# A two-layer graph network on one core: the last product by seven quarter products, with an order of its own for each end

## The chip, the core and the metric

The kernel runs on one core of one Trainium2 chip. Its engines are TensorE (PE, with its weight loads shown apart as PEld), VectorE (DVE), ScalarE (ACT), GpSimd (POOL) and SyncE (SP), which here issues nearly all transfers. The metric is the device time of one execution in microseconds, lower is better.

## The reference

64 graphs of 256 nodes with 256 features, and an integer 256 x 256 adjacency for each, all in float32, pass two blocks. The first has two graph attentions and a feed-forward, the second an eight-head attention with a value weight for each relation, and a feed-forward:

```python
h = gat(x, adj, W1, a1); h = gat(h, adj, W2, a2)       # softmax over axis 1, masked by adj > 0
h = ln(x + h, g_ln1, b_ln1)
y = ln(h + relu(h @ w_ff1 + b_ff1) @ w_ff2 + b_ff2, g_ln2, b_ln2)
q, k = y @ Wq + bq, y @ Wk + bk                        # 8 heads of 32
attn = softmax(q k^T / sqrt(32))
out = sum over r of (attn * (adj == r)) @ (y @ Wv[r] + bv[r])
c = ln(y + out @ Wo + bo, g1, beta1)
d = ln(c + gelu(c @ W1 + b1) @ W2 + b2, g2, beta2)     # W1 256x1024, W2 1024x256
```

## The kernel before

`binary` does the work; it holds for an adjacency of zeros and ones, and `general` follows only if another value was seen. One graph is cut into about 180 pieces, small functions kept under names in a dictionary (`graph`, L762). `L` loads, `G` does both graph attentions and the first layer norm's sums, `F` the first feed-forward, the second norm and q and k, `A` the heads, `T` the output projection, the third norm, the second feed-forward, the last norm and the store.

The order of the work is written out by hand. `PERIOD` (L43) lists all pieces, each with a lag: `F.f0/2` in period n is that piece of graph n - 2. The loop at L791 goes through 69 periods (64 graphs and the largest lag, 5), and runs of each list entry only what exists. Nothing reorders it: each engine meets its instructions, and SP its DMA issues, in this order, and waits at semaphores where data or a buffer is not ready. The first periods and the last ones run the same list with most entries missing.

Names that are needed below:

- `seven_products` (L429): a product of 2 x 2 blocks by seven block products in place of eight. Pieces a to e are on PE and write PSUM banks X, Z and Y; pieces k1 to k4 take a bank out first, p1 to p3 add a bank to what was taken. It needs four sums of blocks of the left side (`S`, made on POOL by `combine`, L414) and of the right side (weights, made once, by `differences`, L153). It is used for both feed-forwards' first product (`F.h*`, `T.h*`) and the values (`A.v*`).
- `out` (L513), pieces `F.f0`, `F.f1`, `T.f0`, `T.f1`: the second product of a feed-forward, plain, eight accumulated matmuls for each half of the nodes, 256 columns wide. A float32 matmul is two instructions in the trace.
- `F.r0` to `r3` and `T.ge0` to `ge3`: bias and relu or gelu on ACT (L509).
- `layernorm` (L354): `ln` (add and statistics on DVE), `rs` (root on POOL), `nm` (DVE); `scaled` (L386): `ra`, `rb`, times weight and plus bias on POOL (L392, L399). A to D are the four norms.
- `turned` (L322): `dt` turns a tile by a transposing DMA, `dm` moves its halves by two DMAs, the join (`c*`, `mg*`, L345) copies on ACT or POOL.
- Heads: `sc` scores, `mx`, `ex` (L685, into a tile `p`, five buffers), `rz`, `sp` (POOL, L698), `dt`, `dm`, `mg`, `pm` (times adjacency, DVE, L713), `o` (L721), `oc`; `T.wo` projects.
- PSUM: all pieces take their tiles from one pool of eight banks (`mm_tile`, L109).
- Setup: `joint_weights` (L215) builds `wx`; `fold_ff`, `column_bias` and `scale_rows` put a norm's weight and bias into the next product's weights (L260 to L267). These stand ahead of the periods; `after` (L307) loads and folds the rest after periods 1 and 2.

## Time and profile before

| what | us |
|---|---|
| median of 3 runs | 3156.15 (3155.87 to 3160.32) |
| the profiled execution | 3158.29 |
| its span | 3156.4 |
| PE busy / DVE / ACT / POOL | 3048.8 / 2459.1 / 2555.5 / 2122.4 |
| mean granted clock of PE | 0.986 |
| bytes by DMA | 449 MB, 142 GB/s |
| matmuls of L517 (both second products) | 466.2 + 455.0 |
| matmuls of L495 (both first products) | 967 |

The span is the time from the first to the last instruction; the time of the execution has a little around it. In the lines below a group is: source line, engine, operation, output <- inputs, shapes, count, then its busy time and the mean of one in ns, then the idle time of its engine just before it and what ended most of that. Matmuls overlap in the pipeline, so the mean of one is longer than the step from one to the next. A tile's letter is the norm whose output it belongs to: `ff_c` and `hid_c` are the second feed-forward's (`T`), `ff_a` the first's.

### The profile page before, as it was taken

To read this page: it belongs to the slowest core of one execution; us is meant where nothing else is said; L and a number is where in the kernel's file an instruction comes from. 1 tells how busy PE (TensorE), PEld (TensorE's weight loads), DVE (VectorE), ACT (ScalarE), POOL (GpSimd) and SP (SyncE) were. 2 spreads that over 40 slices of the span, in tenths; PEclk is the share of its full clock that TensorE was granted. 3 is DMA by queue.
4 is the path that set the end of the run, shared out by engine and by line. 5 is a ranking of instruction groups with operands and counts; after the bars stand their busy time and mean duration, and the time that the engine had idled before them with its cause. 6 is when DMAs were issued, how large, how long until landed. Compare 5 with 4: busy or idle time off the path is not lost.

```text
span 3156.4 us, 64811 instructions
## 1 busy us (share of the span) xinstructions
PE 3048.8 (97%) x21734; PEld 2613.1 (83%) x21734; DVE 2459.1 (78%) x5231; ACT 2555.5 (81%) x5822; POOL 2122.4 (67%) x2990
## 2 busy tenths in 40 slices
PE   5799999999999999999999999999999999999996
PEld 4678888888888888888888888888888888888875
DVE  3578888888888888888887888888888888888763
ACT  1478888888888888888888888888888888888874
POOL 2457667667766766766766776766776676676664
PEclk8899999999999999999999999999999999999998
DMA  4477777778678677777677777777777767777663
GB/s 133 87 140 151 142 148 147 146 142 153 145 148 151 143 143 154 144 148 147 146 143 150 148 145 146 151 141 149 151 143 147 152 141 148 151 143 145 143 128 68
DMA packets 1022849, 449.14 MB, mean 142 GB/s; under 512 B 770960, under 2 KB 1020816, under 8 KB 1022512
## 3 DMA queue, kind: packets, MB, share of 16 engines
q1 hardware_dynamic: 1021248, 442.70, 70.0%
q8 instruction: 175, 2.87, 0.4%
q0 software_dynamic: 976, 1.72, 0.4%
q14 instruction: 162, 1.33, 0.1%
q10 hardware_dynamic: 288, 0.52, 0.1%
HBM read 58.87 MB, written 16.78 MB: 24 GB/s over the span
## 4 chain that ended last, share of the span: by engine, by line
PE 85%; DMA 5%; ACT 3%; DVE 3%; POOL 2%; issue 2%; SPq 0%; ACTq 0%; POOLq 0%; DVEq 0%
PE ff_a L517 13%; PE ff_c L517 12%; PE o L721 7%; PE hX_a L495 7%; PE hX_c L495 6%; PE sc L671 4%; PE vX L645 3%; PE k L632 3%; PE wo L740 3%; PE wh L544 3%; PE q L632 3%; PE gat_b L597 3%; PE hY_c L495 3%; PE gat_a L597 3%; PE hY_a L495 3%; DMA halves_p<-pairs_p 3%
## 5 line engine op out<-in xcount | busy, mean ns | idle before, releaser
L345 ACT COPY pm<-halves_p 128x1024 uint16<-128x1024 uint16 x384 | 516.6, 1346 | 119.6 <-DMA halves_p<-pairs_p 118.6
L713 DVE TENSOR_TENSOR pm<-pm,adj 128x512 f32<-128x512 f32 x512 | 465.4, 926 | 87.4 <-POOL pm L345 63.6
L517 PE MATMUL ff_c<-w_L_gnn_W,hid_c 128*128 128x256 f32 x2048 | 466.2, 381 | 8.4 <-ACT hid_c L509 8.4
L517 PE MATMUL ff_a<-w_L_gnn_w_ff,hid_a 128*128 128x256 f32 x2048 | 455.0, 380 | 2.2 <-ACT hid_a L509 2.2
L517 PEld LDWEIGHTS ff_a<-w_L_gnn_w_ff,hid_a 128*128 128x128 f32 x2048 | 390.6, 191 | 56.4 <-ACT hid_a L509 2.9
L517 PEld LDWEIGHTS ff_c<-w_L_gnn_W,hid_c 128*128 128x128 f32 x2048 | 385.9, 191 | 61.2 <-ACT hid_c L509 10.2
L721 PE MATMUL o<-pm,v 128*32 128x256 f32 x4096 | 249.9, 383 | 1.3 <-ACT pm L345 0.9
L509 ACT ACTIVATE hid_a<-hid_a,col_L_gnn_b_ff 128x256 f32<-128x256 f32 x512 | 218.4, 512 | 12.4 <-DVE hid_a L477 12.4
L345 POOL COPY pm<-halves_p 128x1024 uint16<-128x1024 uint16 x128 | 172.1, 1345 | 81.5 <-DMA halves_p<-pairs_p 74.7
L509 ACT ACTIVATE hid_c<-hid_c,col_L_gnn_b 128x256 f32<-128x256 f32 x512 | 218.3, 496 | 4.9 <-DVE hid_c L477 2.0
L721 PEld LDWEIGHTS o<-pm,v 128*32 128x32 f32 x4096 | 120.7, 110 | 98.5 <-issue 16.7
L425 POOL TENSOR_TENSOR S_a<-cols_a 128x128 f32<-128x128 f32 x128 | 58.5, 457 | 179.2 <-ACT cols_a L345 179.2
L495 PEld LDWEIGHTS hX_a<-cols_a,f_L_gnn_w_ff 128*128 128x128 f32 x1024 | 126.0, 194 | 41.4 <-DVE s_B L573 24.3
L495 PE MATMUL hX_a<-cols_a,f_L_gnn_w_ff 128*128 128x128 f32 x1024 | 144.6, 285 | 13.3 <-ACT cols_a L345 9.2
L671 PE MATMUL sc<-kT,qT 32*128 32x256 f32 x2048 | 149.1, 403 | 1.5 <-ACT qT L642 1.5
L495 PE MATMUL hX_a<-S_a,f_L_gnn_w_ff 128*128 128x128 f32 x1024 | 138.2, 278 | 9.1 <-ACT hid_a L474 9.0
L345 ACT COPY cols_y<-halves_y_y 128x1024 uint16<-128x1024 uint16 x64 | 86.5, 1352 | 74.5 <-DMA halves_y_y<-pairs_y_y 74.4
L632 PE MATMUL k<-cols_y,w_L_gnn_Wk 128*128 128x256 f32 x512 | 127.2, 393 | 18.5 <-ACT cols_y L345 18.5
L495 PE MATMUL hX_c<-S_c,f_L_gnn_W 128*128 128x128 f32 x1024 | 141.7, 281 | 2.2 <-ACT hid_c L474 2.2
L495 PEld LDWEIGHTS hX_a<-S_a,f_L_gnn_w_ff 128*128 128x128 f32 x1024 | 130.0, 192 | 16.7 <-ACT hid_a L474 12.6
L495 PEld LDWEIGHTS hX_c<-cols_c,f_L_gnn_W 128*128 128x128 f32 x1024 | 134.2, 191 | 11.6 <-ACT cols_c L345 4.2
L495 PEld LDWEIGHTS hX_c<-S_c,f_L_gnn_W 128*128 128x128 f32 x1024 | 124.2, 191 | 23.0 <-issue 19.6
(2747 smaller groups left out, 8837.6 us busy)
## 6 DMA issues: line engine op xcount, KB each, us to landing
halves_p<-pairs_p SPq DMA_DIRECT2D x1024, 128.0 KB, 3.3
xT<-in_xT SPq DMA_DIRECT2D x64, 256.0 KB, 4.0
adj<-in_adjT SPq DMA_DIRECT2D x64, 256.0 KB, 4.0
x<-in_x SPq DMA_DIRECT2D x64, 256.0 KB, 3.3
halves_y_a<-pairs_y_a SPq DMA_DIRECT2D x128, 128.0 KB, 3.3
halves_y_y<-pairs_y_y SPq DMA_DIRECT2D x128, 128.0 KB, 3.2
halves_y_c<-pairs_y_c SPq DMA_DIRECT2D x128, 128.0 KB, 3.0
out<-res_d SPq DMA_DIRECT2D x64, 256.0 KB, 2.4
```

The lines of the kernel that those rows point to most:

```text
L345: copy(into().bitcast(U16).rearrange("p (n s) -> p s n", s=2), t["halves"].rearrange("p s k q -> p s (k q)"),)
L495: nc.tensor.matmul(ps[:, f * P : (f + 1) * P], weights()[0][:, factor, f * P : (f + 1) * P], left, start=start and f == 0, stop=f == FC // ...
L509: nc.scalar.activation(tiles["hid"][:, f, :], tiles["hid"][:, f, :], func, bias=b1[:, f : f + 1])
L517: nc.tensor.matmul(tiles["ff"][:, i, :], tiles["hid"][:, f, nodes(i)], weights()[2][:, f, :], start=(f == 0), stop=(f == FC - 1),)
L544: nc.tensor.matmul(t["whp", j], tiles["xT"][:, c, nodes(j)], wx[:, c, :], start=(c == 0), stop=(c == KC - 1),)
L597: nc.tensor.matmul(ps, t["s"][:, j, nodes(i)], t["whz"][:, j, :width], start=(j == 0), stop=(j == NT - 1),)
L632: nc.tensor.matmul(t[key + "p"][:, o, :], w[:, c, nodes(o)], tiles["cols"][:, c, :], start=(c == 0), stop=(c == KC - 1),)
L645: nc.tensor.matmul(ps, left, wv[:, factor, :], start=start, stop=True, skip_group_check=True)
L671: nc.tensor.matmul(t["sc", g, hh][:, i, :], qkv["q"][hd, g, nodes(i)], qkv["k"][hd, g, :], start=True, stop=True,)
L713: nc.vector.tensor_tensor(pm[:, 1, :], pm[:, 0, :], tiles["adj"], ALU.mult)
L721: nc.tensor.matmul(ps[hh * DH : (hh + 1) * DH, :], qkv["v"][:, j, d0 : d0 + DH], t["pm", (g, hh)][:, r, j * N : (j + 1) * N], start=(r == ...
L740: nc.tensor.matmul(t["wo"][:, i, :], t["oT"][:, c, nodes(i)], late["wo"][:, c, :], start=(c == 0), stop=(c == KC - 1),)
```

## The change

- The second feed-forward's second product goes through `seven_products`: pieces `T.fa` to `T.fe` on PE, with 128 columns each, into three PSUM banks. `T.u0` to `u3` make the four sums of the hidden tile's blocks on POOL; the sums of `W2` are made once (`S.p2`). `T.fk*` and `T.fp*` take out and add the banks on DVE; the first takes the residual along.
- The last norm: `ln` only makes statistics; `nm` multiplies by the weight and `rb` by the root with the bias added, both on DVE (`weighted`, `finished`). `T.raD` is gone. The pieces of a period go from 181 to 194.
- `PERIOD` is a new list, run 59 times. `START` (446 entries) and `END` (538) are lists of their own, with each piece's graph written out (negative: from the end).
- Setup becomes pieces `S.*` within `START`, and the late weights' loads (`S.lw`) stand near its front.
- Tiles `p` have four buffers, `S` two; the bank sums of the fold of q and k share one tile.

```diff
 PERIOD = """
-A.dt10/3 F.hk3/2 A.pm01/4 T.hd/5 A.ex13/3 A.mg13/4 A.dm12/3 A.pm02/4 F.hd/2 A.sc0/3 F.hp3/2
...
+G.nmA/1 A.mx13/3 A.rz12/3 F.raB/4 F.sB/3 T.hk3/5 A.mx11/3 A.rz10/3 L.xT/0 T.hp3/5 A.vp2/4 A.dm02/4
+A.pm03/4 G.wh0/0 A.mg02/4 T.hd/5 A.ex13/3 T.hp2/5 G.wh1/0 A.ex11/3 A.sp12/3 A.dm00/4 G.wc0/0
+A.sp10/3 G.wc1/0 A.ve/4 A.pm01/4 F.dtA/1 A.mg00/4 F.dmA/1 F.f1/2 A.pm02/4 G.eA/0 A.pm00/4 T.rbC/5
+F.rbB/4 A.vk4/4 T.he/5 T.ge0/5 A.rz11/3 A.pm11/4 A.rz13/3 A.dt10/3 F.lnB/2 A.sc0/3 A.o0/4 T.ge1/5
+A.mx00/3 G.lrA/0 F.cA/1 T.hk4/5 A.o1/4 T.ge2/5 A.sp11/3 A.sp13/3 A.mx02/3 A.dt12/3 F.ha/1 A.oc0/4
+T.ge3/5 L.adj/0 A.oc1/4 F.sA/1 A.ex00/3 F.hb/1 A.mx03/3 G.away/0 A.dm10/3 A.dm12/3 F.rsB/2 F.hk1/1
+F.hk2/1 T.wo/4 A.mx01/3 G.adA/0 A.mg10/3 T.u0/5 F.hp1/1 T.lnC/4 F.hc/1 T.u1/5 A.mg12/3 A.dt13/3
+G.exA/0 F.raA/1 A.dt11/3 F.nmB/2 A.ex03/3 A.dm13/3 G.rzA/0 T.fa/5 F.hk3/1 A.ex02/3 T.rsC/4 T.fb/5
+F.hd/1 T.nmC/4 G.gA0/0 T.u3/5 T.fk1/5 T.fk2/5 A.rz03/3 A.ex01/3 T.u2/5 F.hp2/1 L.x/0 F.hp3/1
+A.mg13/3 A.sp03/3 G.gA1/0 A.pm12/3 G.wd0/0 G.wd1/0 A.dm11/3 A.rz01/3 T.fc/5 A.va/3 A.vb/3 F.dtB/2
+T.fk3/5 A.mg11/3 F.rbA/1 A.sp01/3 F.r0/1 A.pm13/3 T.dtC/4 A.rz02/3 A.vk1/3 G.eB/0 T.fd/5 F.dmB/2
+T.fp1/5 A.vk2/3 G.lrB/0 T.fp2/5 F.cB/2 F.he/1 A.vc/3 T.dmC/4 T.fe/5 A.rz00/3 F.r1/1 G.adB/0
+A.dt03/3 T.cC/4 A.dt01/3 F.q/2 A.vk3/3 G.exB/0 F.hk4/1 A.vp3/3 T.fp3/5 F.qe0/2 F.k/2 A.sp02/3
+T.fk4/5 F.r2/1 T.ha/4 F.qe1/2 A.dm03/3 F.ke0/2 T.hk1/4 T.lnD/5 G.rzB/0 T.nmD/5 A.sp00/3 T.sC/4
+G.gB/0 A.vp1/3 T.hb/4 A.dm01/3 T.rsD/5 A.dt02/3 T.raC/4 F.ke1/2 T.rbD/5 T.hp1/4 A.sc1/2 T.out/5
+A.dt00/3 G.lnA/0 A.mg03/3 T.hk2/4 F.r3/1 A.mg01/3 A.mx12/2 A.mx10/2 A.vd/3 G.rsA/0 T.hc/4 A.pm10/3
+F.f0/1 A.ex12/2 A.ex10/2
 """.split()
+START = """
+G.away:0 L.adj:2 S.lw:0 S.v0:0 L.adj:1 G.wh0:0 G.wh1:0 G.wc0:0 G.wc1:0 G.eA:0 G.lrA:0 G.adA:0
+S.f0:0 G.exA:0 G.rzA:0 G.gA0:0 G.gA1:0 G.wd0:0 G.wd1:0 S.f1:0 G.eB:0 G.lrB:0 S.f2:0 L.xT:1 G.wh1:1
+G.adB:0 G.wh0:1 L.xT:2 G.exB:0 G.rzB:0 G.wc0:1 G.wc1:1 G.gB:0 G.wh0:2 G.eA:1 G.away:1 G.lrA:1
+G.lnA:0 G.rsA:0 G.nmA:0 G.adA:1 F.dtA:0 F.raA:0 G.exA:1 S.p2:0 S.v1:0 G.wh1:2 S.q0:0 G.wc0:2
...
+END = """
+A.dm02:-4 F.raB:-4 A.vp2:-4 T.hk3:-5 A.pm03:-4 F.sB:-3 A.mx11:-3 A.ve:-4 A.rz12:-3 A.mg02:-4
...
+T.out:-2 T.fe:-1 T.fk4:-1 T.lnD:-1 T.rsD:-1 T.nmD:-1 T.rbD:-1 T.out:-1
+""".split()
...
+    def column_biases(*of, norm):
...
+    def fold_ff(setup, key, ff, norm):
+        half, t = FC // 2, {}
+        def products():
+            def block(c, i):
+                return ff()[0][:, BLOCKS[c, i // half], nodes(i % half)]
+            t["ps"] = column_biases((block, FC), norm=norm())
+        def scales():
+            add_to(ff()[1], t["ps"])
+            scale_rows(lambda c: [ff()[0][:, BLOCKS[c, h], :] for h in range(2)], norm())
+        setup[f"S.{key}0"], setup[f"S.{key}1"] = products, scales
...
+    def out_factors(name):
+        return half_factors(
+            name, FC // 2 * P,
+            lambda c, h: t[name][c * FF // 2 : (c + 1) * FF // 2, nodes(h)].rearrange(
+                "(f p) d -> p f d", p=P
+            ),
         )
...
-    fold_ff(w1, ff0[1], norms[0])
-    differences()
...
-    for w, bias in ((wk, bk), (wq, bq)):
-        column_bias(bias, norms[1], lambda c, i, w=w: w[:, c, nodes(i)], KC)
-        scale_rows(lambda c, w=w: [w[:, c, :]], norms[1])
-    nc.gpsimd.tensor_scalar(bq, bq, QSCALE, 1.0, ALU.mult, ALU.mult)
...
-        late["ff1"] = w1, column("L1_gnn_b1"), weight("L1_gnn_W2", FC)
+        w2, late["out_differences"] = out_factors("L1_gnn_W2")
+        late["w"] = w1, w2
+    def late_rows():
+        late["b1"] = column("L1_gnn_b1")
         for n in ("L1_gnn_g1", "L1_gnn_beta1", "L1_gnn_b2", "L1_gnn_g2", "L1_gnn_beta2"):
             rows[n] = row(t[n], n)
-    def after(period):
-
-        if period == 1:
-            fold_values()
-            late_weights()
-            join_biases(("L0_gnn_b_ln1", "L0_gnn_b_ff2"), ("L0_gnn_b_ln2", "L1_gnn_bo"))
-        elif period == 2:
-            fold_ff(*late["ff1"][:2], norms[2])
-            late["differences"]()
-            join_biases(("L1_gnn_beta1", "L1_gnn_b2"))
+    def ff1():
+        return late["w"][0], late["b1"], late["w"][1]
+    setup = {
+        "S.f2": differences, "S.q0": queries, "S.q1": scaled_queries,
+        "S.v0": value_difference, "S.v1": values, "S.v2": scaled_values, "S.v3": value_differences,
+        "S.lw": late_weights, "S.lr": late_rows, "S.l2": lambda: late["differences"](),
+        "S.j1": lambda: join_biases(("L0_gnn_b_ln1", "L0_gnn_b_ff2"), ("L0_gnn_b_ln2", "L1_gnn_bo")),
+        "S.j2": lambda: join_biases(("L1_gnn_beta1", "L1_gnn_b2")),
+        "S.p2": lambda: late["out_differences"](),
+    }
+    fold_ff(setup, "f", lambda: ff0, lambda: norms[0])
+    fold_ff(setup, "l", ff1, lambda: norms[2])
...
+        def weighted():
+            tiles["res"] = work.tile([P, NT, D], F32, tag="res", name=f"res_{name}", bufs=3)
+            for i in range(NT):
+                nc.vector.scalar_tensor_tensor(
+                    tiles["res"][:, i, :], tiles["acc"][:, i, :], tiles["mv"][:, i, 0:1],
+                    rows[last[0]], ALU.subtract, ALU.mult,
+                )
+        def finished():
+            for i in range(NT):
+                nc.vector.scalar_tensor_tensor(
+                    tiles["res"][:, i, :], tiles["res"][:, i, :], tiles["rstd"][:, i : i + 1],
+                    rows[last[1]], ALU.mult, ALU.add,
+                )
+        do[f"{stage}.ln{key}"], do[f"{stage}.rs{key}"] = sums, root
+        if last:
+            do[f"{stage}.nm{key}"], do[f"{stage}.rb{key}"] = weighted, finished
+        else:
+            do[f"{stage}.nm{key}"] = norm
         return tiles
...
+        def sums(n):
+            if n == 0:
+                h = work.tile([P, 3, FC // 2, P], F32, tag="H", name=f"H_{name}", bufs=1)
+                tiles["H"] = h[:, 0], h[:, 1], hidden(1, 0), h[:, 2]
+            blocks = [hidden(i, h) for i in range(NT) for h in range(2)]
+            engine = nc.gpsimd if ('POOL', 'POOL')[1] == "POOL" else nc.vector
+            add_sums(engine, blocks, tiles["H"], [n])
+        def out_of(ps, factor, left, start):
+            for f in range(FC // 2):
+                nc.tensor.matmul(
+                    ps, left[:, f, :], weights()[2][:, factor, f * P : (f + 1) * P],
+                    start=start and f == 0, stop=f == FC // 2 - 1, skip_group_check=True,
+                )
+        def result(i, h):
+            if "ff" not in tiles:
+                tiles["ff"] = work.tile([P, NT, D], F32, tag="acc", name=f"acc_{name}", bufs=2)
+            return tiles["ff"][:, i, nodes(h)]
+        def begin_result(i, h, ps):
+            nc.vector.tensor_tensor(result(i, h), ps, tiles["res"][:, i, nodes(h)], ALU.add)
+        seven_products(
+            do, stage, "h", name, *by_columns(tiles), into, begin_hidden, hidden, FC // 2 * P
+        )
         for n in range(FC // 2):
             do[f"{stage}.{act}{n}"] = partial(activate, n)
-        for i in range(NT):
-            do[f"{stage}.f{i}"] = partial(out, i)
+        if not seven:
+            for i in range(NT):
+                do[f"{stage}.f{i}"] = partial(out, i)
+            return
+        for n in range(4):
+            do[f"{stage}.u{n}"] = partial(sums, n)
+        seven_products(
+            do, stage, "f", name, hidden, lambda n: tiles["H"][n - 1], out_of,
+            begin_result, result, P,
+        )
...
-            p = t["p", h] = work.tile([P, 2, NT, NT, 64], F32, tag="p", name=f"p_{b}_{g}{hh}", bufs=5)
+            p = t["p", h] = work.tile([P, 2, NT, NT, 64], F32, tag="p", name=f"p_{b}_{g}{hh}", bufs=4)
...
-        feed_forward(do, "T", f"c{b}", c, lambda: late["ff1"], "ge", AF.Gelu)
-        d = layernorm(do, "T", "D", f"d{b}", lambda: (c["ff"], c["res"]))
-        scaled(do, "T", "D", f"d{b}", d, "L1_gnn_g2", "L1_gnn_beta2")
+        feed_forward(do, "T", f"c{b}", c, ff1, "ge", AF.Gelu, seven=True)
+        d = layernorm(
+            do, "T", "D", f"d{b}", lambda: (c["ff"],), ("L1_gnn_g2", "L1_gnn_beta2")
+        )
...
+    lags = max(lag for _, lag in order)
+    def run(piece, b):
+        if piece.startswith("S."):
+            return setup.pop(piece)()
+        if b not in graphs:
+            graphs[b] = {}
+            graph(b, graphs[b], load(graphs[b], b))
+        graphs[b].pop(piece)()
     with tc.manual_schedule(engines={E.PE, E.DVE, E.Activation, E.Pool, E.SP}):
-        for period in range(B + max(lag for _, lag in order)):
-            if 0 < period < B:
-                graphs[period] = {}
-                graph(period, graphs[period], load(graphs[period], period))
+        for entry in START:
+            piece, b = entry.split(":")
+            run(piece, int(b))
+        for period in range(lags, B):
             for piece, lag in order:
-                if do := graphs.get(period - lag, {}).pop(piece, None):
-                    do()
-            after(period)
-        assert not any(graphs.values()), graphs
+                run(piece, period - lag)
+        for entry in END:
+            piece, b = entry.split(":")
+            run(piece, B + int(b))
+        assert not setup and not any(graphs.values()), graphs
```

## The prediction

> **What bounds the kernel now.** I read the page's busy times first, then a table of busy time by stretch, then the timeline of PE inside one period and at both ends. The page says PE 97%, but a busy matmul row is not yet a full PE, so I look for what a period costs.
>
> ```profile
> PE 3048.8 (97%) x21734; PEld 2613.1 (83%) x21734; DVE 2459.1 (78%) x5231; ACT 2555.5 (81%) x5822; POOL 2122.4 (67%) x2990
> PEclk8899999999999999999999999999999999999998
> ...
> L517 PE MATMUL ff_c<-w_L_gnn_W,hid_c 128*128 128x256 f32 x2048 | 466.2, 381 | 8.4 <-ACT hid_c L509 8.4
> ```
>
> The timeline of PE, in the middle of the run (start, length, group, count):
>
> ```profile
> 1455.83 3.62 PE L517 MATMUL ff_c<-w_L_gnn_W,hid_c 128*128 128x256 f32 x16
> ...
> 1502.48 3.62 PE L517 MATMUL ff_c<-w_L_gnn_W,hid_c 128*128 128x256 f32 x16
> 1505.93 0.59 PE L645 MATMUL vX<-f_Wv,S_y 128*128 128x256 f32 x2
> ...
> 1510.04 1.05 PE L495 MATMUL hX_c<-cols_c,f_L_gnn_W 128*128 128x128 f32 x8
> 1510.93 1.06 PE L495 MATMUL hZ_c<-cols_c,f_L_gnn_W 128*128 128x128 f32 x8
> 1511.86 1.99 PE L632 MATMUL k<-cols_y,w_L_gnn_Wk 128*128 128x256 f32 x8
> ```
>
> One graph to the next takes 1502.48 - 1455.83 = 46.65 us. Matmuls overlap, so I price one by the distance between group starts: sixteen of 256 columns in 3.45 us are 216 ns each; eight of 128 columns in 0.89 us, or in 0.93 with what follows, are 112 ns. At such prices a graph's matmuls add up to 46.1 us, so a period is PE work, with nothing between. From the sixth graph's ff_c (471.7) to the fifty-ninth's (2956.0) the mean period is 46.87: only 0.22 us of each is a stall. The stretches say the same, and where PE does starve:
>
> ```profile
> 0.00:240.00 240.00, 174.39 (x996) 145.80 (x997) 135.70 (x296) 115.73 (x282) 109.10 (x162) 0.87 0.55 121
> 240.00:2956.00 2716.00, 2710.47 (x19593) 2332.13 (x19592) 2211.60 (x4694) 2312.78 (x5276) 1897.94 (x2667) 1.00 0.74 147
> 2956.00:3157.00 201.00, 163.94 (x1149) 135.13 (x1147) 111.84 (x243) 127.02 (x265) 115.34 (x163) 0.93 0.52 107
> ...
> 1400.30:1446.95 46.65, 46.65 (x340) 40.20 (x339) 38.05 (x82) 40.17 (x92) 32.78 (x47) 1.00 0.73 150
> ```
>
> Columns after the length: PE, PEld, DVE, ACT, POOL busy, granted clock, DMA share, GB/s. The first and third stretch hold 66 + 37 us of idle PE, and the clock there is 0.87 and 0.93. In all, 3156.4 - 64 x 46.65 = 171 us lie above pure PE work: some 13 are stalls in the middle, the rest are the ends and setup. So there are two things to win: PE work per graph, and the ends.
>
> **The change, part by part.**
>
> *PE per graph.* Out go T.f0 and T.f1, 32 matmuls of 256 columns: 32 x 216 = 6.91 us. In come T.fa to T.fe, seven products of four blocks, two instructions each: 56 matmuls of 128 columns. Row: 56 x 112 = 6.27 us. Gain 0.64 us a graph; the floor becomes 46.65 - 0.64 = 46.01.
> The Trainium skill ("TensorE: Matmul & The Clock Gate", section "Back-to-back issue gap") speaks against this: in a stream of weight load and matmul pairs it gives about 81 ns a matmul at 128 columns and about 131 at 512, so narrow matmuls cost far more than their share. Between its two figures 256 columns come to about 98 (an estimate); at that ratio a 128-column one would cost 216 x 81/98 = 179 ns, T.f 10.0 us, and the change would lose 3.1 us a graph, 198 in all. The hX_c and hZ_c rows are the same shape, a new 128x128 weight block each time, and take 112, not 179. I go by the row.
>
> *DVE per graph.* Out: acc_d, 672 ns, and two y_d, 2 x 533: 1.74 us. In: seven adds from PSUM of 128x128. No such row; 128x512 takes 668 and 128x256 takes 414, which continues to 287: 2.01. In: four scalar_tensor_tensor of 128x256 (weighted, finished), no row either. Bounds: 0.41 (the add of that width) to 0.85 (double, as below). I take 0.42: 1.68. DVE goes from 38.05 by +1.95 to 40.0 of 46.0, 87%.
> *POOL per graph.* Out: res_d, 2 x 948 and 1289: 3.19. In: T.u0 to u3, four adds of 128x512, by the nearest row (differences of w_ff, 1297 to 1434) 1.37 each: 5.48. POOL from 32.8 to 35.1, 76%. ACT keeps its 40 us (87%), SP its issues.
>
> ```profile
> L713 DVE TENSOR_TENSOR pm<-pm,adj 128x512 f32<-128x512 f32 x512 | 465.4, 926 | 87.4 <-POOL pm L345 63.6
> L392 POOL TENSOR_TENSOR res_d<-y_d,row_L_gnn_g 128x256 f32<-128x256 f32 x128 | 118.5, 948 | 2.2 <-DVE y_d L377 2.2
> L399 POOL TENSOR_TENSOR res_d<-res_d,row_L_gnn_beta 128x512 f32<-128x512 f32 x64 | 82.5, 1289 | 0.2
> L361 DVE TENSOR_TENSOR acc_d<-ff_c,res_c 128x512 f32<-128x512 f32 x64 | 43.0, 672 | 22.0 <-PE ff_c L517 22.0
> ```
>
> pm, two SBUF inputs, averages 926 ns where the adds from PSUM of its size take 668 to 692. The skill ("GPSIMD Engine Reference", section "1. Specifications") says that POOL shares its SBUF interfaces with DVE and that DVE instructions with two SBUF inputs contend; by that rule more POOL work stretches the four new DVE instructions and pm too. If both doubled against their free rate, DVE would gain 1.7 + 8 x (2 x 0.67 - 0.93) = 5 us and pass PE; by the mean row it is 87%. I go by the row and keep the rule as a rival.
>
> All this is covered by PE's 46 us while no queue runs late. If it does, each late microsecond is PE's.
>
> *The new order and its waits.* New hand-offs between PE and DVE: T.fc stands 0.9 us of matmuls behind T.fk1 and T.fk2, T.fd 0.2 behind T.fk3, T.fe 1.8 behind T.fp2; the adds take 0.29. The old order has such spots as well (A.vc 0.0 behind A.vk2), and stalls 0.22. The p tiles go from five buffers to four. In the new order A.ex02 takes the buffer that A.dt13 frees, with 1.8 us of matmuls (T.fa) between, and a transpose lands 3.2 us after its issue (the nearest such distance before: 7.3). Behind A.ex02 on ACT are A.ex01, then G.wd0 and G.wd1, for which G.eB on PE waits, 3.1 us later. Cost between 0 and 1.4 us a period; I take 0.1. The banks of PSUM: 33 tiles a period through eight, where there were 31; the tightest reuse stays at 0 to 1 us of PE in both orders. Bounds for the whole stall: 0.1 (less than now) and 1.0 (these waits all landing on PE); I take 0.45 against 0.22, nearer to the old order's row. Period 46.46.
>
> *The start.* START issues 118 us of PE work at row prices: G of five graphs 28, F's first product for four 25, its second for three and a half 24, q and k 10, v, sc, o and wo of the first two 16, T.ha to T.hc 5, folds 10. Before, the same amount of matmuls is out at 220. What can now set it is graph 0's chain, in the lengths of the old timeline:
>
> ```profile
> 27.04 1.85 PE L173 MATMUL fold<-col_L_gnn_b_ln,w_L_gnn_Wk 128*128 128x1 f32 x8
> 30.46 3.76 PE L544 MATMUL wh<-wx,xT 128*128 128x260 f32 x8
> 65.36 2.07 PE L495 MATMUL hX_a<-cols_a,f_L_gnn_w_ff 128*128 128x128 f32 x8 [8.87 <-ACT cols_a L345]
> 105.48 3.78 PE L632 MATMUL k<-cols_y,w_L_gnn_Wk 128*128 128x256 f32 x8 [7.78 <-ACT cols_y L345]
> ```
>
> The folds stand ahead of wh on PE; moved behind it, wh starts when wx is built, near 22. Then G 23, to hX 12, the hidden layer 14, ff 8, to k 12, to sc 6, sc to o some 30 (59 before, spread over a period), to T.ha 22, its three pieces 6: 155. With four graphs crowding I take 170, bounds 155 and 190. S.lw, nine loads of 2.25 MB, moves to the front of SP: 4.5 us of issue by the rows of the same loads at 61 to 64. Behind it are L.adj:1 and L.xT:1, not needed before graph 1's wh; hidden behind graph 0's G, at most 5 us if not. Its POOL pieces (S.v3, S.f2, S.p2: 3 + 5 + 5 us by the rows of such differences, and the six loads that S.lr issues on POOL's queue) sit where POOL idles for want of graphs; S.p2 is the only one that is new. So -50 (220 to 170).
>
> *The end.* END holds 118 us of PE work, the old order's like 122, which ran from 2987 on: 169 us. The last graph's chain in old lengths (to hX 10, hidden 10, ff 7, to k 12, to sc 5, to o 25, to T.ha 19, to gelu 9, T.f with its sums 9, to the end 9) is 115. Work and chain alike: I take 145, bounds 130 and 160.
>
> *Sum.* 170 + 59 x 46.46 (the periods between) + 145 = 3056 of span. The profiled execution took 3158.3 with a span of 3156.4, 1.9 around it, and lies 2.1 above the median of 3156.15; so 3056 stands against the median too.
>
> **The rivals.**
> - *Waits eat the gain in the middle.* The p buffers and hand-offs put 0.9 us or more on PE: 170 + 59 x 47.0 + 145 = 3088. For: distances of 0.2 and 1.8. Against: ACT has 6 us free a period.
> - *Ends pack better, no new stall.* 155 + 59 x 46.15 + 133 = 3011. For: in both ends chain and work are of one size. Against: in-order queues with cold clock.
> - *DVE becomes the bound, slower.* With POOL's new sums overlapping them, pm and the four new instructions stretch; DVE then needs 45 of busy time plus waits. It decides from a period of (3162 - 315)/59 = 48.3 us, 2.2 of stall; at 49 it is 3206. Against: pm's mean has to rise from 926 to 1340.
> - *Narrow matmuls cost 179*: a period of 46.65 + 3.1 + 0.45, 315 + 59 x 50.2 = 3277. Against: 7168 of them already run at 112.
>
> **How the numbers follow.** Forecast as summed 0.57 (3030 to 3080), better 0.14, waits 0.20, DVE 0.06, narrow 0.01, and 0.02 for no gain at all within what can be told from no change (0.2%, 6 us). Slower 0.07, same 0.02, faster 0.91. The range takes the bounds together: 155 + 59 x 46.11 + 130 = 3005; above, the waits in the middle together with the slow bound of the start, 190 + 59 x 47.0 + 145 = 3108.
>
> **What would show it.** In the changed profile: fX_c, fY_c, fZ_c groups at 112 ns between starts; a period of 46.0 to 46.6; T.u sums near 1.37; seven DVE adds near 0.29; pm's mean near 926; wh of graph 0 near 22 and PE full from 170 on. Wrong if the period is 47 or more, if pm's mean is above 1.1 us, or if PE waits on ACT p (L685) or the f tiles lead its waits.

## The result, and the profile after

| kernel | median us | ratio to before |
|---|---|---|
| before | 3157.71 (3155.87 to 3160.32) | |
| changed | 3123.83 (3119.28 to 3133.95) | 0.9897 [0.987, 0.9923] |

The forecast was 3056, with a range from 3005 to 3108. The change is faster, by a third of what was forecast. The page of the changed kernel (its profiled execution took 3121.47 us, its span 3119.7):

```profile
PE 3007.0 (96%) x23270; PEld 2629.7 (84%) x23270; DVE 2747.0 (88%) x5744; ACT 2548.7 (82%) x5822; POOL 2290.2 (73%) x3057
PEclk9999999999999999999999999999999999999998
...
L922 DVE TENSOR_TENSOR pm<-pm,adj 128x512 f32<-128x512 f32 x512 | 565.6, 1123 | 19.3 <-POOL pm L484 12.2
L702 PE MATMUL fX_c<-f_L_gnn_W,hid_c 128*128 128x128 f32 x1536 | 207.2, 278 | 7.3 <-ACT hid_c L678 5.1
```

PE is 41.8 us less busy, and the span is only 36.7 us shorter, although START alone ends some 30 us earlier than the same work did. `pm` has gone from 926 to 1123 ns. The table by stretch shows where PE starves now (columns as before: PE, PEld, DVE, ACT, POOL busy, clock, DMA share, GB/s):

```profile
0.00:240.00 240.00, 199.07 (x1225) 169.82 (x1226) 164.87 (x353) 139.55 (x344) 135.83 (x197) 0.94 0.62 136
240.00:2956.00 2716.00, 2679.18 (x21003) 2350.74 (x21002) 2484.29 (x5167) 2312.51 (x5279) 2051.05 (x2727) 1.00 0.71 147
2956.00:3120.00 164.00, 128.73 (x1045) 109.15 (x1043) 97.82 (x225) 96.62 (x201) 103.31 (x135) 0.93 0.49 104
```

In the middle PE was idle for 5.5 us before and is idle for 2716.0 - 2679.2 = 36.8 us now; DVE is busy for 91% of it. The waits of PE from 400 to 2400 us (engine, line, what it waited for: us in total, times, longest) name two groups, DVE's results and `cols_y`:

```profile
PE gat_a L800 <- DVE whz_A L794: 9.6, 18, 1.0
PE fX_c L702 <- DVE acc_c L713: 7.0, 23, 0.3
PE q L835 <- ACT cols_y L484: 5.9, 10, 1.1
PE fZ_c L702 <- DVE hid_a L637: 2.9, 4, 1.3
```

One period of PE's timeline shows such waits in their places (start, length, group, count, in brackets the wait ahead of it):

```profile
1429.76 0.70 PE L800 MATMUL gat_a<-whz_A,s_A 128*128 128x258 f32 x2 [0.62 <-DVE whz_A L794]
1431.06 1.57 PE L800 MATMUL gat_a<-whz_A,s_A 128*128 128x258 f32 x6 [0.59 <-DVE whz_A L794]
...
1432.95 1.13 PE L702 MATMUL fX_c<-f_L_gnn_W,H_c 128*128 128x128 f32 x8 [0.31 <-DVE acc_c L713]
...
1441.12 1.99 PE L835 MATMUL q<-cols_y,w_L_gnn_Wq 128*128 128x256 f32 x8 [1.05 <-ACT cols_y L484]
```

For the sum I cut the run as the forecast did. The first piece of the second product, F.f0, is the last PE work of a period and takes 3.5 us, so START ends one period before the end of graph 4's F.f0, and END begins with the end of graph 62's. For the changed kernel that is 189.5 + 59 x 46.81 + 168.5 = 3119.8, against 170 + 59 x 46.46 + 145 = 3056:

| part | forecast | measured | off by |
|---|---|---|---|
| START | 170 | 189.5 | +19.5 |
| 59 periods | 59 x 46.46 = 2741 | 59 x 46.81 = 2762 | +21 |
| END | 145 | 168.5 | +23.5 |

The shortest period is 45.67 us, 0.34 less than the forecast floor. So the stall in a period is 1.14 us, not 0.45: the middle could have won 59 x (46.81 - 45.67) = 67 us more.

### The profile page after: what moved, and what is told of

Same layout as the page of the kernel before. It is cut to its first block, busy times and chain, and to the rows that moved or that the text cites. A ratio compares the mean times of both kernels' runs of the same rounds, so it can differ in the third digit from the quotient of the medians.

```text
span 3119.7 us, 68789 instructions
## 1 busy us (share of the span) xinstructions
PE 3007.0 (96%) x23270; PEld 2629.7 (84%) x23270; DVE 2747.0 (88%) x5744; ACT 2548.7 (82%) x5822; POOL 2290.2 (73%) x3057
## 4 chain that ended last, share of the span: by engine, by line
PE 68%; DVE 12%; DMA 8%; issue 3%; ACT 3%; POOL 1%; SPq 1%; DVEq 0%; ACTq 0%; POOLq 0%
PE ff_a L686 11%; PE hX_c L661 6%; PE o L930 5%; PE fX_c L702 5%; PE hX_a L661 4%; PE sc L880 3%; PE q L835 3%; PE hY_c L661 3%; PE k L835 3%; PE gat_b L800 3%; PE vX L848 3%; PE wh L747 3%; DVE pm L922 2%; PE wo L949 2%; DMA adj<-in_adjT 2%
## 5 line engine op out<-in xcount | busy, mean ns | idle before, releaser
L922 DVE TENSOR_TENSOR pm<-pm,adj 128x512 f32<-128x512 f32 x512 | 565.6, 1123 | 19.3 <-POOL pm L484 12.2
L930 PE MATMUL o<-pm,v 128*32 128x256 f32 x4096 | 235.3, 381 | 5.5 <-POOL p L907 2.4
L702 PE MATMUL fX_c<-f_L_gnn_W,hid_c 128*128 128x128 f32 x1536 | 207.2, 278 | 7.3 <-ACT hid_c L678 5.1
L514 POOL TENSOR_TENSOR rstd_a<-var_a,neghalf 128x2 f32<-128x2 f32 x64 | 45.0, 702 | 222.5 <-DVE var_a L510 222.5
L702 PEld LDWEIGHTS fX_c<-f_L_gnn_W,hid_c 128*128 128x128 f32 x1536 | 192.8, 192 | 13.2 <-ACT hid_c L678 5.8
L584 POOL TENSOR_TENSOR S_c<-cols_c 128x128 f32<-128x128 f32 x128 | 58.3, 455 | 128.4 <-ACT cols_c L484 128.4
L800 PE MATMUL gat_a<-whz_A,s_A 128*128 128x258 f32 x512 | 134.9, 400 | 18.2 <-DVE whz_A L794 15.4
L747 PE MATMUL wh<-wx,xT 128*128 128x260 f32 x512 | 136.0, 390 | 12.5 <-DVE wx L372 10.1
L702 PE MATMUL fY_c<-f_L_gnn_W,H_c 128*128 128x128 f32 x1024 | 137.3, 278 | 3.8 <-POOL H_c L584 3.8
L661 PE MATMUL hX_c<-cols_c,f_L_gnn_W 128*128 128x128 f32 x1024 | 135.8, 276 | 2.7 <-ACT cols_c L484 2.7
```

What stands on the lines that cost most here:

```text
L661: nc.tensor.matmul(ps[:, f * P : (f + 1) * P], weights()[0][:, factor, f * P : (f + 1) * P], left, start=start and f == 0, stop=f == FC // ...
L702: nc.tensor.matmul(ps, left[:, f, :], weights()[2][:, factor, f * P : (f + 1) * P], start=start and f == 0, stop=f == FC // 2 - 1, skip_gr ...
L747: nc.tensor.matmul(t["whp", j], tiles["xT"][:, c, nodes(j)], wx[:, c, :], start=(c == 0), stop=(c == KC - 1),)
L800: nc.tensor.matmul(ps, t["s"][:, j, nodes(i)], t["whz"][:, j, :width], start=(j == 0), stop=(j == NT - 1),)
L922: nc.vector.tensor_tensor(pm[:, 1, :], pm[:, 0, :], tiles["adj"], ALU.mult)
L930: nc.tensor.matmul(ps[hh * DH : (hh + 1) * DH, :], qkv["v"][:, j, d0 : d0 + DH], t["pm", (g, hh)][:, r, j * N : (j + 1) * N], start=(r == ...
```

## The experiments

All times are medians, beside runs of the kernel before on the same chip. Those runs' own medians lie between 3154 and 3158, so a few us between two rows of this table say nothing.

| run | what it is | us | ratio to before |
|---|---|---|---|
| e_adj5 | five adj buffers, L.adj earlier | 3148.42 | 0.9969 [0.9961, 0.9977] |
| e_p5 | five p buffers | 3126.95 | 0.9899 [0.9877, 0.9921] |
| e_plain | plain second product, new lists | 3139.19 | 0.9939 [0.9922, 0.9955] |
| e_nosums | T.u sums left out | 3110.01 | 0.9847 [0.983, 0.9863] |
| e_pairs3 | three `pairs` buffers | 3054.5 | 0.9675 [0.9659, 0.9691] |
| e_pstart | START from the period's list | 3167.5 | 1.0039 [1.0029, 1.0048] |
| e_pend | END from the period's list | 3131.0 | 0.992 [0.9904, 0.9937] |
| e_normpool | last norm back on POOL | 3196.28 | 1.0125 [1.0107, 1.0144] |
| e_plain_pairs3 | e_plain with three `pairs` | 3121.6 | 0.9885 [0.9866, 0.9905] |
| b_pairs3 | kernel before, three `pairs` | 3139.57 | 0.9946 [0.9928, 0.9964] |
| e_win_s1 | three `pairs`, one `s` | 3055.6 | 0.9678 [0.966, 0.9695] |
| e_win_away | three `pairs`, two adj | 3051.53 | 0.9666 [0.9649, 0.9682] |
| e_win_warm | e_win_s1, PE kept busy at the start | 3053.65 | 0.9677 [0.9655, 0.9699] |
| e_pairs3_udve | e_pairs3, sums on DVE | 3043.29 | 0.9647 [0.9623, 0.967] |
| e_udve | sums on DVE, two `pairs` | 3102.63 | 0.9839 [0.9815, 0.9864] |
| e_best | e_win_s1, sums on DVE | 3046.82 | 0.9649 [0.9632, 0.9665] |

**First suspects: late loads, p buffers, the product, its sums.**

```diff
 e_adj5
-    tag="adj", name=f"adj_{b}", bufs=4
+    tag="adj", name=f"adj_{b}", bufs=5      # and L.adj/0 straight behind L.xT/0
 e_p5
-    p = t["p", h] = work.tile(..., bufs=4)
+    p = t["p", h] = work.tile(..., bufs=5)
 e_plain
-    T.fa ... T.fe, T.fk1 ... T.fp3, T.u0 ... T.u3
+    T.f0, T.f1
 e_nosums
-    h = work.tile([P, 3, FC // 2, P], F32, tag="H", name=f"H_{name}", bufs=1)
+    h = hconst                               # T.u0 to u3 do nothing
```

> The changed kernel with a fifth buffer for the adjacency tile, and L.adj/0 moved to stand behind L.xT/0 at the front of PERIOD. To make room, beta1 and beta2 of the second block are not loaded (g1 and g2 stand in their place). In the changed kernel a period costs 46.81 us where PE alone needs 45.67; G.away waits 57 us in all for the adjacency, whose load waits for the last pm of four graphs before. Theory 'late load' (this wait makes DVE late and so PE): the wait falls to about nothing, DVE idle turns into slack, the period falls to about 46.2, the time by 30 us or more. Theory 'DVE load' (DVE's 42.7 us of work a period, stretched by POOL's new sums, is what PE waits for): the wait goes, but at most 10 us of the time with it. Theory 'p buffers' (four in place of five): nothing, within 6 us.

> The changed kernel with five p buffers again (room made by not loading beta1 and beta2, as in e_adj5), its lists as they are. Theory 'p buffers', the one that the prediction named: the ACT waits ahead of ex go and the time falls by 20 us or more. Theories 'late load' and 'DVE load': within 6 us of the changed kernel.

> The changed kernel with the second product of the second feed-forward plain again (T.f0 where T.fa stood, T.f1 where T.fe stood, T.lnD where T.fk4 stood, no T.u sums, W2 as before); lists, setup, ends and the last norm on DVE as changed. PE needs 0.64 us or so more a graph: its floor is about 46.3. Theory 'DVE load': DVE loses 1.3 us of its own and some 1.5 of stretching, stalls fall from 1.14 to about 0.3, the period is 46.6 and the time some 10 us below the changed kernel: the product brings nothing. Theory 'late load': stalls stay near 1.1, the period is 47.4, the time 35 us above the changed kernel.

> The changed kernel without the T.u sums: the products read one constant tile in place of the sums of hidden blocks, so POOL does 5.8 us a graph less and all else is as changed. Theory 'DVE load', by contention: pm's mean falls from 1123 ns towards 950, DVE from 42.7 to about 40.5 us a period, the period to about 46.1, the time by 35 us. Theory 'late load': pm's mean falls as well, but the wait of G.away stays and the time falls by 12 us at most.

e_p5 makes no difference (3127 against 3124): the p buffers, my forecast's first suspect, are not it. (It also leaves out beta1 and beta2 to make room, as several runs below do; so that does not make a kernel faster either.) e_plain says that the seven quarter products bring 15 us of the 38 (59 x 0.64) that their PE rows promise. e_nosums wins 14, and in its profile the waits on DVE (gat_a, fX_c) leave PE's list, but q's wait for cols_y grows (the profiled execution, 3129 us, was the slowest of five, so by how much is not sure). e_adj5 is the telling miss. DVE's `away` waited 42.6 us for adj in 2000 us. A fifth buffer and an earlier issue took that wait away, and the kernel became 25 us slower (which of the two edits did that was not parted), with one wait leading PE's list:

```profile
PE q L837 <- ACT cols_y L486: 24.6, 29, 2.1
```

cols_y is a joined turn, so I looked at the queue that issues the turns. SP issues in order. Its waits in the changed kernel from 400 to 2400 us (SPq is SP's queue of issues, L469 is `dt`, L477 is `dm`):

```profile
SPq L469 <- DMA halves_p<-pairs_p: 249.0, 219, 3.4
...
SPq L469 <- DMA halves_y_a<-pairs_y_a: 44.5, 46, 2.3
...
SPq L469 <- DMA halves_y_y<-pairs_y_y: 34.9, 42, 1.1
...
SPq L469 <- DMA halves_y_c<-pairs_y_c: 20.7, 40, 0.8
```

Here a `dt` waits until the two halves of an earlier turn have landed, since only then is one of the two `pairs` buffers free. That is 349 us in 2000, or 8.2 us of each period, and everything behind it on SP stands still meanwhile, L.adj too. From the issue and landing times in the same stretch of the trace a turn holds its buffer 7.95 us on average: some 3.35 to its landing, 0.45 until SP comes to `dm`, 0.6 between the two halves, the rest for them to land. Eleven turns a graph on two buffers are 11 x 7.95 / 2 = 43.7 us of each 46.81. The buffers are 93% taken, more than DVE.

**The third buffer.**

```diff
-            t["pairs"] = work.tile([P, 2, 4, P], U16, tag="pairs", name=f"pairs_{name}", bufs=2)
+            t["pairs"] = work.tile([P, 2, 4, P], U16, tag="pairs", name=f"pairs_{name}", bufs=3)
```

> Three buffers for `pairs` (the turned tile between dt and its two dm transfers) in place of two; the biases beta1 and beta2 are not loaded for it (the scale rows stand in their place). Turn-chain theory: SP issues in order, and a dt waits there for a free `pairs` buffer while all issues behind it stand still (247 us of 2000 us); with a third buffer the halves land earlier, q's wait for cols_y and ACT's waits for halves (110 us for pm) shrink by half or more, the period falls from 46.81 to 46.5 or less, and the run takes 3108 or less (-15 or more against the changed kernel's 3124). DVE-lateness theory: the stall is DVE's load, stretched by POOL's sums; SP's waits are waiting time in any case, and the run stays within 6 us of 3124.

It takes 3054.5 us: 69 less than the changed kernel, where I had written 15 or more. SP's waits in the same stretch (L470 is `dt`, L478 `dm`), PE's only one, and DVE's for adj are now:

```profile
SPq L478 <- DMA pairs_y_a<-y_a: 97.0, 44, 3.9
SPq L478 <- DMA pairs_p<-p: 80.5, 100, 2.3
...
SPq L470 <- DMA halves_p<-pairs_p: 4.9, 14, 0.8
```

```profile
PE q L836 <- ACT cols_y L485: 4.9, 7, 1.3
```

```profile
DVE away L740 <- DMA adj<-in_adjT: 0.5, 1, 0.5
```

The 349 us are 5, and with them went the wait for adj and the waits of PE on DVE, though DVE is as busy as before (42.4 us a period against 42.8) and `pm` as slow (1111 ns). So DVE was late mostly because SP had been late (what the sums add to it comes below). The period is 45.86, its median 45.67, the floor. A turn now holds its buffer 8.37 us: 11 x 8.37 / 3 = 30.7 of 45.9, 67%.

**Is the third buffer a gain of its own, and what is the product worth with it?**

> The kernel before with three `pairs` buffers, nothing else. Turn-chain theory: before, PE's own work (46.65 us a period) covers the turns although SP waits for `pairs` 275 us in 2000 us as well; only 0.22 us of a period is a stall, so at most 13 us are there to win: 3141 to 3156. If the third buffer is a gain of its own that the kernel before had missed as well, it is 30 or more faster (3125 or less).

> The plain second product (T.f0, T.f1; no T.u sums) in the new lists, with three `pairs` buffers; beta1 and beta2 are not loaded for it. Turn-chain theory: once the turns no longer bind, the product is worth what the rows of the kernel before say, 0.64 us of PE and no stall: a period of 46.5 to 46.65, so 3054.5 + 59 x 0.7 = about 3096 (3088 to 3104). If the product itself had been the trouble (its sums, its contention), the plain one with three buffers is no slower than 3065.

In the kernel before it brings 15 us (3154.13 beside it), and the period is 46.65 with no wait left: the old stall of 0.22 a period, 13 us, and a little more. So the old order lived with two buffers that were 92% taken (11 x 7.87 / 2 = 43.3 of 46.87). PE's work was 1 us longer there; what its order of the turns adds to that was not tried. The plain product with three buffers takes 3121.6, where I expected 3096: its period stays at 46.91, just what it is in e_plain with two (the 18 us between these two runs lie in the ends). Yet in e_plain the two buffers were 94% taken too (11 x 8.01 / 2 = 44.1 of 46.91) and SP waited 316 us in 2000 for them. So the share taken does not by itself tell the cost: some 44 us of turns did no harm in the middle beside a PE that needs 46.3 us, and did beside one that needs 45.7 and a DVE with 42.8; where between them it begins is not shown. The profile shows what holds the plain product's period up: each has one wait of PE that has nothing to do with turns.

```profile
1433.92 0.70 PE L842 MATMUL vX<-f_Wv,S_y 128*128 128x256 f32 x2 [0.32 <-ACT v L858]
```

Against it the seven products are worth 3121.6 - 3054.5 = 67 us, more than 59 x 0.64 = 38; the middle has 59 x (46.91 - 45.86) = 62 of it. The wait of 0.32 costs 0.59 a period with the slow restart behind it (0.17 up to the start of this group and 0.10 to that of the next, by the usual distances of group starts). Without it the plain product's period is 46.32, so the product's own gain is 46.32 - 45.67 = 0.65: my 0.64.

**The ends.**

```diff
 e_pstart, e_pend
-START = ...; END = ...
+START = the list of PERIOD for periods 0 to 4, setup after periods 1 and 2; END = the same for the last five
```

> START is replaced by the list of a period for its first five periods (missing entries left out), with the setup pieces where the kernel before had them. If the start's own order is what brought the 30 us there (220 to 189.5), this run is 30 slower than the changed kernel: about 3154, and the fifth ff_a is back near 263. If the gain came from the setup's earlier loads or from the first graphs' work alone, less than 12 slower.

> END is replaced by the list of a period for its last five periods (missing entries left out). My account of the changed kernel says that its END (168.5 us) brought nothing against the kernel before (169): this run stays within 8 us of 3124. If the own order of the end does work, and only the slower clock and the turns' transfers took its gain back, this run is 20 or more slower (3144 or more).

START's list is worth 3167.5 - 3123.8 = 44 us (its part of the profiled run, which is 10 us above the median, goes from 189.5 to 240 without it; the same work was out at 220 before). The edit takes back the order of the pieces and the place of the setup together, so it cannot say which of them brought the gain. END's list is worth 7 by the medians, which the spread of either kernel covers (3119 to 3134 and 3123 to 3136), and 12 in its part of the two profiled runs (180 against 168.5).

**The last norm on POOL.**

> The last norm's weight and bias go back to POOL (nm on DVE as a tensor_scalar, raD and rbD on POOL, as in the kernel before, with four `y` buffers for it); the biases beta1 and beta2 are not loaded for it. DVE loses about 1.5 us a period and POOL gains 3.2 (35.3 to 38.5 of 46.8). DVE-lateness theory with DVE's own load as the cause: the period falls by 0.2 or more, 3112 or less. If it is POOL's share of the common port that makes DVE late (more POOL work, slower pm), the period stays or rises: 3124 to 3145. Turn-chain theory: POOL also joins the halves of two heads (mg0), so nothing is gained: within 8 of 3124.

It took 72 us more, as none of the theories said, and the profile shows a wait on POOL that my edit lengthened from 7.7 us to 76.9 in 2000: res_b waits for the store of res_d.

```profile
POOL res_b L557 <- DMA out<-res_d: 76.9, 42, 3.5
```

That wait is the likely cause, not a tested one. So the run says nothing on DVE's load; the next one does.

**Where the sums should be made.**

```diff
-            engine = nc.gpsimd if ('POOL', 'POOL')[1] == "POOL" else nc.vector
+            engine = nc.gpsimd if ('POOL', 'DVE')[1] == "POOL" else nc.vector
```

> e_pairs3 (three `pairs` buffers, beta1 and beta2 not loaded) with the T.u sums on DVE in place of POOL. DVE as the bound, with the turns out of the way: the sums leave POOL (35.4 to about 30 us a period, pm's mean from 1.11 to about 1.05 as in e_nosums) and add four adds of 128x512 to DVE (0.7 to 1.2 us each): DVE from 42.4 to 39.8 + 2.8 to 4.8 = 42.6 to 44.6 of 45.9. If DVE has the room that e_pairs3 shows, 3050 to 3075; if the DVE rival of my forecast is close (late hand-offs cost PE from about 44 us of load on), 3085 or more.

> The recorded kernel with the T.u sums on DVE and the two `pairs` buffers kept; nothing left out. Turn-chain theory: the turns still bind (as in e_nosums, 3110), so 3100 to 3120, with PE's waits for cols_y as the longest. If DVE's stretch by POOL was the main cause after all, the sums' move alone gives 3065 or less.

The groups of the sums by engine (line, engine, operation, shapes, count, busy, mean ns, idle ahead), first of the changed kernel, then of e_pairs3_udve:

```profile
L584 POOL TENSOR_TENSOR H_c<-H_c,hid_c 128x512 f32<-128x512 f32 x64 | 93.4, 1459 | 4.8
```

```profile
L585 DVE TENSOR_TENSOR H_c<-H_c,hid_c 128x512 f32<-128x512 f32 x64 | 44.3, 692 | 0.0
L923 DVE TENSOR_TENSOR pm<-pm,adj 128x512 f32<-128x512 f32 x512 | 537.4, 1068 | 10.6 <-POOL pm L485 6.4 <-ACT pm L485 4.2
```

DVE takes on four adds of some 0.7 us, and its busy time falls: 42.04 us a period against 42.36. The sums cost DVE as much on POOL as if it made them itself, and POOL's are twice as long. Where DVE paid for them shows in two of its groups, which have one wide input each: y_c and whz_A (first the changed kernel with a moment of its timeline, then e_pairs3_udve).

```profile
L519 DVE TENSOR_SCALAR y_c<-acc_c,mv_c,rstd_c 128x256 f32<-128x256 f32 x128 | 106.8, 873 | 2.9 <-POOL rstd_c L514 2.7
L794 DVE TENSOR_SCALAR whz_A<-wh_A,grz_A 128x258 f32<-128x258 f32 x128 | 102.3, 842 | 2.3
...
1429.35 1.65 DVE L794 TENSOR_SCALAR whz_A<-wh_A,grz_A 128x258 f32<-128x258 f32 x2
1429.45 1.40 POOL L584 TENSOR_TENSOR H_c<-hid_c,H_c 128x512 f32<-128x512 f32 x1
```

```profile
L520 DVE TENSOR_SCALAR y_c<-acc_c,mv_c,rstd_c 128x256 f32<-128x256 f32 x128 | 48.1, 418 | 1.2 <-POOL rstd_c L515 1.0
L795 DVE TENSOR_SCALAR whz_A<-wh_A,grz_A 128x258 f32<-128x258 f32 x128 | 41.6, 368 | 2.3
```

The second of the two whz_A instructions ends only some 0.15 us after POOL's add, and gat_a on PE waits for it (the 0.59 at 1431.06 above). These two groups are 2 x (0.455 + 0.474) = 1.9 us a graph; `pm`, 1123 to 1068 ns, is 0.4. The period is 45.67 throughout. With two `pairs` buffers the same move wins only 21 us (e_udve; q waits for cols_y again, and the period is 46.33 in the profiled execution, the fastest of four), so the turns were the larger cause and this the smaller.

**Versions with nothing left out.** The third buffer needs 2 KB per partition. e_win_s1 takes it from `s`:

```diff
-            s = t["s"] = work.tile([P, NT, N], F32, tag="s", name=f"s_{step}{b}", bufs=2)
+            s = t["s"] = work.tile([P, NT, N], F32, tag="s", name=f"s_{step}{b}", bufs=1)
```

> Nothing left out: three `pairs` buffers, paid for by one buffer for `s` (the graph attention's scores) in place of two; in START, G.eA, G.lrA and G.adA of graphs 2 and 3 stand behind G.gB of the graph before. Turn-chain theory: as e_pairs3 in the middle, since in a period s_A is read by gA1 well ahead of eB's next s: 3050 to 3075 (the start may lose up to 10). If the one buffer puts eB's scores behind gA1 on the path, the period goes to 46.3 or more: 3085 to 3110.

e_win_away takes it from two adj buffers, since the byte mask `away` does for the heads as well:

```diff
-            nc.vector.tensor_tensor(pm[:, 1, :], pm[:, 0, :], tiles["adj"], ALU.mult)
+            nc.vector.scalar_tensor_tensor(
+                pm[:, 1, :], tiles["away"].rearrange("p t i -> p (t i)"), 1.0, pm[:, 0, :],
+                ALU.mult, ALU.mult,
+            )
```

> Nothing left out: three `pairs` buffers, paid for by two adj buffers in place of four; the heads are multiplied by the byte mask `away` (kept for five graphs, 1 where adj is 0), with the two relations' value weights changed over, by scalar_tensor_tensor in place of tensor_tensor. pm's free rate in that form is not shown by any row here: if it is that of the tensor_tensor (mean about 1.1 us with POOL beside it), 3050 to 3075; if it is slower by 0.3 us or more (8 a period, DVE from 42.4 to 44.8), DVE is late again and the run takes 3090 or more.

> Nothing left out: e_win_s1 (three `pairs` buffers, one for `s`) with the T.u sums on DVE. If both edits hold as they did apart (a period of 45.67 with no wait on PE, POOL at 31), 3040 to 3050. If one buffer of `s` needs the room that the sums take on DVE, 3055 or more.

All three are as expected: 3055.6 and 3051.5, with `pm` at 1103 and 1110 ns in the two forms, and 3046.8 with the sums on DVE. In e_best PE is busy for the whole of the middle:

```profile
240.00:2884.00 2644.00, 2644.00 (x20972) 2345.86 (x20971) 2432.99 (x5390) 2298.57 (x5268) 1794.85 (x2487) 1.00 0.74 151
```

It runs as 192.1 + 59 x 45.67 + 162.6 = 3049.2 (span 3049.0).

**The slow clock at the start.**

```diff
+        warm = mm_tile("warm", (P, P))
+        for _ in range(30):
+            nc.tensor.matmul(warm, ident, ident, start=True, stop=True)
         for entry in START:
```

> e_win_s1 with 30 idle matmuls (ident by ident, into a bank that nobody reads) on PE between the product that builds wx and graph 0's wh, where PE waits from 11.9 to 21.4 us. In e_win_s1 the groups after that wait run at twice their length of the middle (wh 3.7 us against 1.76, gat_a 3.6 against 1.75), at a granted clock of 0.70 to 0.81 up to 60 us. If that slow clock comes of the wait before it and is what my start's sum left out, wh, the folds and gat_a of graph 0 take half, and the start ends 3 to 7 us earlier (the fifth ff_a at 226 to 230 in place of 233.3). If the first loads (xT of graph 1, waited for at 38.6) set the start, the groups are short and ff_a stays at 231 to 235. If the slow clock has nothing to do with the wait, the groups stay long.

The filler ran at full speed and ended 3.03 us ahead of wh, and wh is still as slow: the edit left most of the wait that it was meant to fill. First the timeline, then stretches, whose third number from the end is the granted clock:

```profile
11.33 6.86 PE L1016 MATMUL warm<-ident 128*128 128x128 f32 x60
21.23 3.74 PE L750 MATMUL wh<-wx,xT 128*128 128x260 f32 x8 [3.03 <-DVE wx L375]
...
38.71 3.47 PE L750 MATMUL wh<-wx,xT 128*128 128x260 f32 x8 [3.41 <-DMA xT<-in_xT]
42.02 1.89 PE L803 MATMUL gat_b<-whz_B,s_B 128*128 128x256 f32 x8
...
52.65 4.19 PE L803 MATMUL gat_a<-whz_A,s_A 128*128 128x258 f32 x8 [2.16 <-DVE whz_A L797]
```

```profile
17.82:21.23 3.41, 0.38 (x5) 0.18 (x3) 3.31 (x12) 0.00 (x0) 1.37 (x2) 1.00 0.90 181
21.23:24.64 3.41, 3.41 (x8) 2.46 (x9) 0.88 (x3) 0.38 (x1) 0.00 (x0) 0.50 1.06 318
...
48.54:51.95 3.41, 1.95 (x18) 1.84 (x16) 2.12 (x4) 1.25 (x5) 3.33 (x3) 1.00 0.62 154
51.95:55.37 3.42, 2.65 (x6) 1.70 (x7) 3.28 (x6) 0.59 (x3) 2.95 (x3) 0.50 0.77 228
55.37:58.78 3.41, 2.41 (x7) 1.30 (x6) 2.65 (x12) 2.06 (x5) 0.22 (x1) 0.50 0.01 5
58.78:62.19 3.41, 3.41 (x17) 3.41 (x18) 2.91 (x4) 0.98 (x3) 3.33 (x6) 0.50 0.00 0
62.19:65.61 3.42, 3.42 (x31) 3.38 (x31) 1.20 (x3) 2.06 (x6) 2.67 (x5) 1.00 0.60 91
```

Each of these slow groups stands behind a wait of 2.2 to 3.4 us, and runs at half the clock. The Trainium skill ("TensorE: Matmul & The Clock Gate", section "What's actually happening") says that the clock is halved after an idle window of about 3.4 us and released after about as long a busy one. The group at 38.71 fits (3.3 us slow, then full), and so does wh: PE was busy for 0.38 us of the 3.41 ahead of it. The one at 52.65 came after a wait of only 2.16 us. In the clock record of this run the clock changes only at steps of 3.41 us, and the stretches above are cut there: it fell after a step with PE busy for 1.95 us of 3.41, stayed low through steps with 2.65 and 2.41, and came back after a full one. So a wholly idle step is not needed here, and a partly busy one does not release the clock; how such a step is weighed is not shown. The time, 3053.65 against 3055.6, can't be told from no change, and the fifth ff_a at 230.4 lies where two of my three expectations meet. Whether the slow clock sets the end of START was not settled by this run.

## Why the prediction was wrong, point by point

Three terms of the sum were too small, by some 20 us each: the stall in the middle, for which I had named the wrong waits, and both ends, whose PE work I had priced at the rate of the middle.

- **PE's price was right, its floor a little high.** Groups of eight 128-column matmuls, timeline of e_best:

```profile
1443.76 1.06 PE L705 MATMUL fX_c<-f_L_gnn_W,hid_c 128*128 128x128 f32 x8
1444.65 1.06 PE L705 MATMUL fZ_c<-f_L_gnn_W,hid_c 128*128 128x128 f32 x8
1445.55 1.06 PE L705 MATMUL fY_c<-f_L_gnn_W,H_c 128*128 128x128 f32 x8
```

  0.89 and 0.90 us for eight: 112 ns, as the row said, and not the 179 that the prediction worked out from the Trainium skill's two figures. The floor is 45.67 instead of 46.01. The product's gain came out as summed (0.65 by e_plain_pairs3); the other 0.33 is between the old order's 46.65 and the new one's 46.32 with the plain product, which I had not asked about.
- **The stall in a period, 0.45 us, is the term that failed in the middle (it was 1.14).** The measured stall lies above even my upper bound, 1.0, because the bounds were drawn around p buffers and PE's hand-offs. I counted engines, and SP's issues as free, and never counted how long the two `pairs` buffers are held: 43 us of each period already before. A third buffer alone takes 0.95 of the 1.14 away, the sums' move the other 0.19. The profile of before shows SP waiting for halves 275 us in 2000; I had passed over SP's waits because SP always waits for something. Shortening PE's work by 1 us met a resource that had 3 to spare. Why the new list stalls on it before it is full is not shown.
- **DVE at 40.0 us was too low (42.8), and did not bind.** The adds from PSUM were right (275 ns against 287). The four weighted and finished instructions were not: 526 and 733 ns against 420, which is 0.84 us a graph; `pm` grew by 0.197 x 8 = 1.58 us, and whz_A, whose code the change does not touch, by 2 x (0.842 - 0.358) = 0.97 (some groups fell). That more POOL work slows DVE, the rule that I had put among the rivals, was right in kind, but I had looked for it in the wrong instructions: without the sums (e_nosums) DVE needs 39.8 us, mostly because y_c and whz_A take half their time, while `pm` still takes 1053 ns and the four new ones 552 and 689. What stretches those is not shown. Of my signs of being wrong, `pm` above 1.1 us came true and pointed at DVE as the bound; still e_pairs3, with `pm` at 1111 ns, has a stall of only 0.19, and e_win_s1 runs near its floor with DVE at 42.3 of 45.8.
- **START, 170: 189.5.** Graph 0's chain was right up to the scores (wh at 22.04, sc at 98.3 where the sum gives 97). From sc to o I took 30 us and it was 47, but PE was busy for 44.9 us of the 48 from 98 to 146: it was not waiting on the chain, it had the other graphs' work to do. (From o to T.ha it was 31.6 for 22, with PE idle for 8.) I had priced all of START's PE work at 118 us, at the middle's rate; in the profile PE is busy for about 150 us of its 190. Most of that is the clock, which my own table showed at 0.87 there: by the trace's clock record and, where it is empty (up to 38 us), by the matmuls' lengths (wh 3.94 us against 1.76), PE was busy for 45 us at half the clock, which costs 23 of the 32. The other 9 stay open.

```profile
45.00:60.00 15.00, 12.25 (x52) 9.73 (x52) 10.75 (x24) 2.84 (x9) 8.32 (x7) 0.73 0.33 89
60.00:75.00 15.00, 13.47 (x80) 12.22 (x79) 11.35 (x25) 9.93 (x24) 6.22 (x10) 0.82 0.28 46
...
100.00:120.00 20.00, 19.06 (x112) 16.82 (x113) 13.09 (x35) 16.72 (x49) 10.91 (x19) 0.92 0.63 119
```

- **END, 145: 168.5.** The same mistake (PE busy 133 us for work priced at 118; 14 us at half the clock cost 7 of the 15), with 35 us of idle PE. With the turns freed it takes 161 to 163, so some 7 of the 23 are the turns; the rest stays open.
- **The p buffers** were no cause (e_p5), and **the narrow matmuls** neither.
- **The range's upper end, 3108,** was not the bounds taken together: it has END at 145, not at its bound of 160. With that it would have been 3123, by luck next to the result, for the stall would still have been put down to other waits.

That e_win_s1 comes out at 3055.6, the forecast number, is no proof of the sum: its terms are 191 + 59 x 45.80 + 161, so 37 us too little at the ends and 39 too much in the middle cancel.

## What to carry to other kernels

Count a rotating buffer like an engine: uses per period times the time from its issue to its release, divided by the number of buffers. Near the bounding engine's own time it belongs among the bounds, and a change that shortens that engine may find it; whether it costs anything only a run with one more buffer tells (93% taken cost 56 us here, 94% in e_plain nothing in the middle). When several engines wait a little, look for what they share upstream, here one in-order queue; a fix for one of the waits (e_adj5) can make the whole slower. Price the ends of a pipelined kernel by what the ends cost in the profile, not by the steps of its middle.

## What was not expected of the hardware

Adds on POOL cost DVE their own price: four adds of 128x512 took 1.33 to 1.60 us each on POOL and 0.68 to 0.80 on DVE, and with them moved to DVE its busy time fell from 42.36 to 42.04 us a period. The price was paid most by DVE instructions with one wide input: y_c took 873 ns with the adds on POOL and 418 without, whz_A 842 and 368. On PE a wait of 2.16 us was enough for eight matmuls at half rate (4.19 us, where the eight of gat_b took 1.89 at the full clock).
